# A graph network layer on one core: VectorE's program held behind each turning of edges, and a small first indirect DMA on GpSimd

## The chip, the cores and the metric

The kernel runs on one core of one Trainium2 chip. The metric is the device time of one execution in microseconds. The profiler takes one execution; the engines are called PE (TensorE, matrix products), PEld (its weight loads), DVE (VectorE), ACT (ScalarE), POOL (GpSimd) and SP (SyncE, here a queue of DMAs).

## The reference

A layer for 8192 nodes of 256 channels with 131072 edges, sorted by their destination. Each edge's message is the relu of its source node's row plus a product of its 64 attributes; messages are summed by destination. Beside this local part, attention runs in groups of 32 nodes with 4 heads. A dense stage and a layer norm follow.

```python
ea = edge_attr @ w_e + b_e
msg = jax.nn.relu(x[src] + ea)
agg = jax.ops.segment_sum(msg, dst, num_segments=N)
t = x + agg
h_local = jax.nn.relu(t @ w1 + b1) @ w2 + b2
h_local = _bn(h_local + x, bn1_g, bn1_b)
...
attn = jax.nn.softmax(scores, axis=-1)
...
h_attn = _bn(h_attn + x, bn2_g, bn2_b)
out = h_local + h_attn
out = out + (jax.nn.relu(out @ m_w1 + m_b1) @ m_w2 + m_b2)
return _bn(out, bn3_g, bn3_b)
...
x = _layernorm(x + _L0_gnn_ref(...))
```

## The kernel before

The edges are worked in 128 blocks of 1024 (NB, BE), the nodes in 16 chunks of 512 (NCH, CH). For one block:

- GpSimd gathers the source rows with eight indirect DMAs of 128 rows each into the tile `xs` (line 217). For the first two blocks the row numbers come from the tile `srcd`, loaded at the very start, later from `srci`. For the first 20 blocks the rows come from `x`, later from `xb`, a copy with the edge bias added. Six blocks lack one of the eight gathers; its rows come by SP's queue. There are six buffers of `xs`.
- VectorE turns the block's edge attributes, `eaT` (line 288, `edge_transpose`; two buffers, so a turning waits until PE has used the one before the last).
- PE multiplies them with the weights into two banks `pe` (`edge_products`).
- VectorE adds the gathered rows to `pe` in two halves (line 348, line 342 for the six blocks), ScalarE takes the relu (line 352, `edge_messages`).
- VectorE makes the one-hot tile `oh` from the edges' places in the block (line 363, `edge_hot`, two buffers), PE sums messages by it into `pw`.
- ScalarE copies the sums to `ws`, VectorE makes a second one-hot tile (line 402), PE places the sums, `l`, and VectorE adds them to the chunk's `xT` (line 422, `edge_place`).

For one chunk there is the attention: products of queries, keys and values (`vn`, line 609), scores copied by ScalarE into `pr`, then VectorE's softmax: maximum `mx` (line 635), subtraction (638), exponential on ScalarE (639), sum `sm` (642), reciprocal (643), product (645), four transposes into the tile `bd` (649). PE multiplies `bd` with `vn`. The dense stage has two layers that add to `hA` (lines 672 and 701), two more with `m` and `zT` (lines 707, 719), transposes, the addition to `xn` which gives `y` (732), statistics (734, 735) and the normalisation (742, 744). The last chunk's dense stage is cut by columns (line 775 and on).

What sets the order: PE's order is that of the program text, in which a planner interleaves blocks and chunks by hand-set times. For VectorE and ScalarE the same holds up to block 24 (NV, the flag `stated`). From there on a scheduler of the framework orders them, by its own estimates of when inputs come. `tc.issue_after(ins)` gives it an edge: instructions named inside the context are issued behind `ins` on the same engine. It is an order alone; no engine waits for a semaphore by it. Each gather is also held behind a PE instruction some ten microseconds ahead of it in the planner's time (`hold_fetches`).

Of the kernel before, what the change touches and what calls it, by code (L numbers as in the profile page):

```python
# [19 lines left out]
P = 128  # L20
N, C, E, ED, H, NPG = 8192, 256, 131072, 64, 4, 32
# [3 lines left out]
NB = E // BE  # L25
NH = 4
WN = P // NH
TJ = BE // NH // P
TB = NH * TJ
QR = 32  # L30
EQ = P // QR
# [12 lines left out]
FETCHED = [44, 54, 64, 76, 86, 98]  # L44
# [40 lines left out]
def gnn_kernel(ctx: ExitStack, tc: tile.TileContext, x, src, dst, edge_attr, w, out):  # L85
    nc = tc.nc

    const = ctx.enter_context(tc.tile_pool(name="const", bufs=1))
# [4 lines left out]
    for b in range(ND):  # L93
        for m in range(EQ):
# [24 lines left out]
    rel = const.tile([P, NB, TB], FP, name="rel")  # L119
# [14 lines left out]
    for v in VECS:  # L134
        n = w[v].shape[0] // P
# [92 lines left out]
    xf_of = {}  # L228
# [48 lines left out]
    stated = [True]  # L277
# [2 lines left out]
        for do in spots:  # L280
            do()

    turned_at = [None]

    def edge_transpose(b):
        ea, g0 = ea_of[b // 2], b % 2 * NH * EQ
        eaT = eaT_of[b] = epool.tile([P, NH * EQ, QR], FP, name="eaT", tag="eaT", bufs=2)
        turned_at[0] = nc.vector.transpose(eaT, ea[:, QR:].rearrange("p (g d) -> p g d", d=ED)[:, g0 : g0 + NH * EQ, :QR]).ins  # L288


    pe_of, msg_of, oh_of, pw_of, newest = {}, {}, {}, {}, {}
# [30 lines left out]
    def edge_messages(b, pairs=range(0, NH, 2), of_pair=range(2)):  # L322

        xs = xs_of[b]
        if b not in msg_of:
            msg_of[b] = xs
        msg = msg_of[b]
        n = 2 if b < NB - 1 else 1
        with ExitStack() as behind:
            if not stated[0]:  # L330
                behind.enter_context(tc.issue_after(turned_at[0]))
            for h in pairs:
                pe = pe_of[b, h]
                for u in of_pair[::n]:
                    hs = slice(h + u, h + u + n)
                    if h + u + n == NH and b in FETCHED:
                        for us, js, rows in (
                            (slice(0, 2), slice(0, TJ - 1), xs[:, h:]), (slice(0, 1), slice(TJ - 1, TJ), xs[:, h:]),
                            (slice(1, 2), slice(TJ - 1, TJ), xf_of[b]),
                        ):  # L340
                            rows = rows[:, None, None, :] if rows is xf_of[b] else rows[:, us, js].rearrange("p u i c -> p i u c")
                            nc.vector.tensor_add(
                                msg[:, h:][:, us, js].rearrange("p u i c -> p i u c"), pe[:, js, us, :], rows
                            )
                        nc.scalar.activation(msg[:, hs], msg[:, hs], AF.Relu)
                        continue
                    for js in [slice(0, TJ)] if n == 2 or h + u < NH - 1 else [slice(j, j + 1) for j in range(TJ)]:
                        nc.vector.tensor_add(  # L348
                            msg[:, hs, js].rearrange("p u i c -> p i u c"), pe[:, js, u : u + n, :],
                            xs[:, hs, js].rearrange("p u i c -> p i u c"),  # L350
                        )
                        nc.scalar.activation(msg[:, hs, js], msg[:, hs, js], AF.Relu)  # L352
        between()

    def edge_hot(b):

        oh = oh_of[b] = epool.tile([P, TB, WN], FP, name="oh", tag="oh", bufs=2)
        with ExitStack() as behind:
            if not stated[0]:
                behind.enter_context(tc.issue_after(turned_at[0]))  # L360
            for t0 in range(0, TB, TB // 2):
                ts = slice(t0, t0 + TB // 2)
                nc.vector.tensor_tensor(
                    oh[:, ts],
                    iota_n[:, None, :WN].to_broadcast([P, TB // 2, WN]),
                    rel[:, b, ts, None].to_broadcast([P, TB // 2, WN]),
                    ALU.is_equal,
                )

    def group_sums(pw, i, b, turns):  # L370
        for h, j in turns:
# [58 lines left out]
    with tc.tile_pool(name="setup", bufs=1) as sp:  # L430
# [16 lines left out]
        for v in VECS:  # L447
            r, n = col[v]
# [475 lines left out]
    with tc.manual_schedule(engines={PE}):  # L924
# [39 lines left out]
        for i, c, a, z in (  # L964
# [20 lines left out]
        b = 0  # L985
        while b < TAIL:
# [77 lines left out]
        p, m = [b, 0], [b, 0]  # L1064
# [10 lines left out]
        while l < NB:  # L1075
# [56 lines left out]
            elif t >= times[2]:  # L1132
                i, k = p
# [17 lines left out]
    with tc.If(wide > 0):  # L1151
        with tc.tile_pool(name="gen", bufs=1) as pool, tc.tile_pool(name="gen_ps", bufs=1, space=PSUM) as ps_pool:
# [11 lines left out]
            with tc.For_i(0, E, P * TE) as e0:  # L1164
                ea = pool.tile([P, TE, ED], FP, name="gea")
# [7 lines left out]
                xs = pool.tile([P, TE, C], FP, name="gxs")  # L1173
                for j in range(TE):
                    nc.gpsimd.indirect_dma_start(
                        out=xs[:, j, :],
                        out_offset=None,
                        in_=xb[:, :],
                        in_offset=bass.IndirectOffsetOnAxis(ap=si[:, j : j + 1], axis=0),
                    )  # L1180
                for j in range(TE):
# [9 lines left out]
                    d = df[:, j : j + 1]  # L1191
# [79 lines left out]
```

## Time and profile before

| what | us |
|---|---|
| median of 3 runs (lowest, highest) | 1311.12 (1310.87, 1316.0) |
| the profiled execution, its own time | 1310.63 |
| its span, first to last instruction | 1308.9 |
| mean granted clock of TensorE | 0.966 |
| PE busy | 1200.1 |
| DVE busy | 792.5 |
| POOL busy | 971.1 |
| ACT busy | 581.6 |

A row of a timeline reads: start, duration of the run of equal instructions, engine, line, operation, output and inputs by the program's names, their number, and in brackets the idle time of the engine ahead of it with what ended it. A row of the windows gives for PE, PEld, DVE, ACT and POOL the busy time and the number of instructions, then the granted clock, the DMA engines' share and GB/s. The duration of several instructions is that of the run of them; neighbours on one engine overlap by some 0.1 us. PE's ends are modelled.

### The profile page before, as it was taken

Reading aid. Unit: us, or ns where it says so; the run is one execution under the profiler, and the core shown is the slowest. Engines: PE = TensorE matmul, PEld = TensorE weight load, DVE = VectorE, ACT = ScalarE, POOL = GpSimd, SP = SyncE. Lnnn points to the kernel's source line nnn. Section 1 sums busy time; section 2 is a strip of 40 time slices with the busy share of each in tenths; the row PEclk is TensorE's granted clock in tenths of the full one; section 3 lists DMA queues with packets and bytes.
Section 4 is the critical chain, followed back from the end, with each engine's and each line's share of the span. In section 5 each row is a group of like instructions: output and inputs, shape, how many; then the busy total and the mean of one; then the engine's idle time right before and its main releaser. Section 6 shows DMA issues by size and latency. Waiting matters only on the chain.

```text
span 1308.9 us, 23368 instructions
## 1 busy us (share of the span) xinstructions
PE 1200.1 (92%) x7671; PEld 722.8 (55%) x7671; DVE 792.5 (61%) x1643; ACT 581.6 (44%) x840; POOL 971.1 (74%) x1026
## 2 busy tenths in 40 slices
PE   4997999899979989798998979979889999999997
PEld 3564556555546545555555545545455655556576
DVE  6676856647446565474746638346565765666563
ACT  3443534445526354352544426425245544545343
POOL 6777777777777777777777777777777777777772
PEclk9998999999999989899999989989989999999999
DMA  8999987767768657667687765866777775777642
GB/s 235 290 298 331 285 218 171 166 174 172 187 151 202 155 152 183 163 159 184 155 187 182 175 167 145 190 162 175 183 186 170 189 182 138 202 160 183 150 133 62
DMA packets 146298, 240.53 MB, mean 184 GB/s; under 512 B 24606, under 2 KB 109756, under 8 KB 145404
## 3 DMA queue, kind: packets, MB, share of 16 engines
q0 software_dynamic: 48864, 133.50, 38.1%
q1 hardware_dynamic: 88828, 98.15, 32.4%
q10 hardware_dynamic: 8480, 7.35, 1.9%
q8 instruction: 62, 1.02, 0.3%
q14 instruction: 64, 0.52, 0.1%
HBM read 222.13 MB, written 16.78 MB: 183 GB/s over the span
## 4 chain that ended last, share of the span: by engine, by line
PE 76%; DMA 9%; issue 5%; DVE 4%; POOL 3%; ACT 1%; SPq 0%; DVEq 0%; POOLq 0%; ACTq 0%
PE at L174 38%; PE pe L174 20%; PE pw L174 9%; PE l L174 5%; DMA xs<-xb,srci 4%; POOL xs L217 3%; DVE xs L348 2%; DMA xn<-in_x_dram 2%; DMA xs<-in_x_dram,srci 1%; PE at L775 1%; PE at L178 1%; DMA ea<-in_edge_attr_dram 1%; PE at L726 1%; ACT xs L352 1%; DMA last_src<-in_src_dram 0%
## 5 line engine op out<-in xcount | busy, mean ns | idle before, releaser
L217 POOL DMA_INDIRECT xs<-xb,srci x858 | 815.4, 950 | 262.3 <-issue 181.4
L352 ACT ACTIVATE xs<-xs 128x1024 f32<-128x1024 f32 (+2 forms) x253 | 263.0, 1045 | 434.0 <-DVE xs L348 357.8
L348 DVE TENSOR_TENSOR xs<-pe,xs 128x1024 f32<-128x1024 f32 (+2 forms) x253 | 300.0, 1204 | 211.1 <-PE pe L174 105.4
L174 PE MATMUL pe<-we,eaT 64*128 64x256 f32 x2048 | 271.1, 401 | 10.1 <-DVE xs L348 8.7
L174 PEld LDWEIGHTS pe<-we,eaT 64*128 64x128 f32 x2048 | 196.1, 194 | 108.5 <-issue 66.3
L174 PE MATMUL pw<-xs,oh 128*32 128x256 f32 x2048 | 142.9, 395 | 32.4 <-issue 20.2
L217 POOL DMA_INDIRECT xs<-in_x_dram,srci x144 | 138.6, 962 | 45.2 <-issue 29.3
L174 PEld LDWEIGHTS pw<-xs,oh 128*32 128x32 f32 x2048 | 61.0, 111 | 113.7 <-issue 54.1
L174 PE MATMUL at<-xT,inT 128*128 128x512 f32 x256 | 121.2, 600 | 1.9 <-ACT xT L578 1.9
L174 PE MATMUL at<-hA,mw 128*128 128x512 f32 (+1 forms) x256 | 114.4, 573 | 0.0
L288 DVE STREAM_TRANSPOSE eaT<-ea 128x512 f32<-128x512 f32 x128 | 89.6, 701 | 36.2 <-PE pe L174 31.4
L174 PE MATMUL at<-m,mw 128*128 128x512 f32 (+1 forms) x256 | 108.9, 570 | 0.0
L174 PEld LDWEIGHTS l<-oh,ws 128*128 128x128 f32 x512 | 74.7, 197 | 20.3 <-issue 16.4
L422 DVE TENSOR_TENSOR xT<-l,xT 128x352 f32<-128x352 f32 (+14 forms) x107 | 43.2, 427 | 70.4 <-PE l L174 70.3
L174 PE MATMUL l<-oh,ws 128*128 128x160 f32 (+4 forms) x512 | 85.8, 308 | 0.0
L174 PEld LDWEIGHTS at<-xT,inT 128*128 128x128 f32 x256 | 47.0, 190 | 60.5 <-issue 50.5
L174 PEld LDWEIGHTS at<-m,mw 128*128 128x128 f32 x256 | 47.0, 190 | 46.5 <-issue 42.2
L707 ACT ACTIVATE m<-at,vec 128x512 f32<-128x512 f32 (+1 forms) x64 | 41.8, 655 | 66.3 <-PE at L174 66.2
L174 PEld LDWEIGHTS at<-hA,mw 128*128 128x128 f32 x256 | 46.1, 190 | 44.0 <-issue 41.0
L591 ACT ACTIVATE qk<-at,vec 128x512 f32<-128x512 f32 x64 | 43.8, 685 | 52.9 <-PE at L174 52.5
L174 PE MATMUL pe<-qk 64*128 64x128 f32 x512 | 42.3, 321 | 23.2 <-DVE xs L348 23.2
L174 PE MATMUL at<-oT,outT 128*128 128x512 f32 x128 | 61.5, 604 | 0.3 <-ACT oT L664 0.3
(157 smaller groups left out, 1282.6 us busy)
## 6 DMA issues: line engine op xcount, KB each, us to landing
ea<-in_edge_attr_dram SPq DMA_DIRECT2D x252, 256.0 KB
xs<-xb,srci POOLq DMA_INDIRECT x858
xf<-xb SPq DMA_DIRECT2D x768, 1.0 KB
xn<-in_x_dram ACTq DMA_DIRECT2D x14, 512.0 KB
out_dram<-y SPq DMA_DIRECT2D x14, 512.0 KB
xp<-in_x_dram SPq DMA_DIRECT2D x10, 512.0 KB
xb<-xp SPq DMA_DIRECT2D x10, 512.0 KB
xp<-in_x_dram SPq DMA_DIRECT2D x3, 1024.0 KB
```

The lines of the kernel that those rows point to most:

```text
L174: mark(ps, nc.tensor.matmul(ps, *args, **kw).ins)
L178: ins = nc.tensor.transpose(ps, *args).ins
L217: nc.gpsimd.indirect_dma_start(out=xs[:, h, j, :], out_offset=None, in_=x if b < NX else xb[:, :], in_offset=bass.IndirectOffsetOnAxis(ap= ...
L288: turned_at[0] = nc.vector.transpose(eaT, ea[:, QR:].rearrange("p (g d) -> p g d", d=ED)[:, g0 : g0 + NH * EQ, :QR]).ins
L348: nc.vector.tensor_add(msg[:, hs, js].rearrange("p u i c -> p i u c"), pe[:, js, u : u + n, :], xs[:, hs, js].rearrange("p u i c -> p i u c"),
L352: nc.scalar.activation(msg[:, hs, js], msg[:, hs, js], AF.Relu)
L422: newest["xT"] = nc.vector.tensor_add(xT, l2[:, :, a - n : z - n], xT).ins
L591: nc.scalar.activation(qk[:, o, :], ps, AF.Identity, bias=v_("in_b", o))
L707: newest["relu"] = nc.scalar.activation(m1[:, o, :], layer(mw1, KC, o, hA), AF.Relu, bias=v_("m_b1", o)).ins
L726: nc.tensor.transpose(ps[:wt, t - t2, k * P : (k + 1) * P], zT[:, k, t * P : t * P + wt], ident)
L775: nc.tensor.matmul(ps[i], wt[:, k, o * P : (o + 1) * P], act[:, k, :], start=(k == 0), stop=(k == nk - 1))
```

## The change

There are two edits.

On GpSimd a column of zeros is written, and an indirect DMA by it reads 32 bytes of row 0 for each partition into a tile `first` that nothing reads. Both stand ahead of the identity matrix and the index rows.

On VectorE the edges of issue are laid otherwise. Before, the messages and the first one-hot tile alone were placed behind the newest turning. Now, from block 24 on, a context is opened behind each turning and closed at the next one (after that one has been named itself): every instruction that the program names between two turnings is issued behind the former, and the latter too. No context is opened for the last block.

```diff
+    zero = const.tile([P, 1], I32, name="zero")
+    nc.gpsimd.memset(zero, 0)
+    first = const.tile([P, 8], FP, name="first")
+    nc.gpsimd.indirect_dma_start(
+        out=first, out_offset=None, in_=x.rearrange("n (a b) -> (n a) b", b=8), in_offset=bass.IndirectOffsetOnAxis(ap=zero, axis=0)
+    )
+
     ident = const.tile([P, P], FP, name="ident")
...
-    turned_at = [None]
+    behind_turn = ctx.enter_context(ExitStack())

     def edge_transpose(b):
...
-        turned_at[0] = nc.vector.transpose(eaT, ea[:, QR:].rearrange("p (g d) -> p g d", d=ED)[:, g0 : g0 + NH * EQ, :QR]).ins
+        ins = nc.vector.transpose(eaT, ea[:, QR:].rearrange("p (g d) -> p g d", d=ED)[:, g0 : g0 + NH * EQ, :QR]).ins
+        behind_turn.close()
+        if not stated[0] and b < NB - 1:
+            behind_turn.enter_context(tc.issue_after(ins))
...
     def edge_messages(b, pairs=range(0, NH, 2), of_pair=range(2)):
...
-        with ExitStack() as behind:
-            if not stated[0]:
-                behind.enter_context(tc.issue_after(turned_at[0]))
-            for h in pairs:
+        for h in pairs:
...
     def edge_hot(b):
...
-        with ExitStack() as behind:
-            if not stated[0]:
-                behind.enter_context(tc.issue_after(turned_at[0]))
-            for t0 in range(0, TB, TB // 2):
+        for t0 in range(0, TB, TB // 2):
```

PE's and SP's instructions and their order are the same before and after. GpSimd has two more. VectorE and ScalarE have the same instructions in another order from about 300 us on. Line numbers of the change are four to seven higher than before (the turning 288 is 295, the message add 348 is 355, the first one-hot tile 363 is 367, xT 422 is 426, vn 609 is 613, mx 635 is 639, bd 649 is 653, zT 719 is 723, y 732 is 736).

The first place on VectorE is the softmax at 1104 to 1112 us of the profile before. Before, from the second zT on:

```order
L719 TENSOR_TENSOR zT<-at,zT 128x512
L643 RECIPROCAL sm<-sm 128x16
L645 TENSOR_TENSOR pr<-pr,sm 128x128 x4
L649 STREAM_TRANSPOSE bd<-pr 32x16x32 x4
L288 STREAM_TRANSPOSE eaT<-ea 128x512
L363 TENSOR_TENSOR oh<-iota_n,rel 128x128 x2
L422 TENSOR_TENSOR xT<-l_10516,xT 128x2x144
L348 TENSOR_TENSOR xs<-pe,xs 128x2x2x256 x2
L732 TENSOR_TENSOR y<-at,xn 128x512 x2
```

And in the change, from the second zT on:

```order
L295 STREAM_TRANSPOSE eaT<-ea 128x512
L367 TENSOR_TENSOR oh<-iota_n,rel 128x128 x2
L426 TENSOR_TENSOR xT<-l_10520,xT 128x2x144
L355 TENSOR_TENSOR xs<-pe,xs 128x2x2x256 x2
L639 TENSOR_REDUCE mx<-pr 128x16
L736 TENSOR_TENSOR y<-at,xn 128x512
L642 TENSOR_TENSOR pr<-pr,mx 128x128 x4
L736 TENSOR_TENSOR y<-at,xn 128x512
L738 BN_STATS st<-y 128x6
L646 TENSOR_REDUCE sm<-pr 128x16
```

The turning and the message add now stand ahead of the whole softmax, of which the two y additions and, further on, the statistics have moved in between; `bd` comes nine rows behind the last one shown. The second place is the next softmax, at 1167 to 1178 us, in the change (before, mx and its subtraction stood ahead of the turning, and the second zT behind bd):

```order
L295 STREAM_TRANSPOSE eaT<-ea 128x512
L367 TENSOR_TENSOR oh<-iota_n,rel 128x128 x2
L426 TENSOR_TENSOR xT<-l_10991,xT 128x2x128
L355 TENSOR_TENSOR xs<-pe,xs 128x2x2x256 x2
L639 TENSOR_REDUCE mx<-pr 128x16
L723 TENSOR_TENSOR zT<-at,zT 128x512
L642 TENSOR_TENSOR pr<-pr,mx 128x128 x4
L406 TENSOR_SCALAR oh_11046<-iota_n,wrow 128x128
L723 TENSOR_TENSOR zT<-at,zT 128x512
L646 TENSOR_REDUCE sm<-pr 128x16
```

The third is where the dense stages of the last two chunks meet, at 1245 to 1247 us. In the change, the addition to xT has moved behind the centring `xc`, both reciprocals and the normalisation of two tiles:

```order
L746 RECIPROCAL rstd<-rstd 128x2
L768 TENSOR_TENSOR xc<-xn,c3row 128x256
L748 TENSOR_SCALAR y<-y,mv,rstd 128x256 x2
L746 RECIPROCAL rstd<-rstd 128x4
L426 TENSOR_TENSOR xT<-l_11614,xT 128x2x112
L748 TENSOR_SCALAR y<-y,mv,rstd 128x256 x4
L355 TENSOR_TENSOR xs<-pe,xs 128x2x2x256
```

Before, `xT` stood ahead of the normalisation and of the second reciprocal, and `xc` some fifteen rows earlier.

More of the change, by code (lines that the diff above doesn't have):

```diff
@@ new lines, in edge_messages @@
+        for h in pairs:
+            pe = pe_of[b, h]
+            for u in of_pair[::n]:
+                hs = slice(h + u, h + u + n)
+                if h + u + n == NH and b in FETCHED:
+                    for us, js, rows in (
+                        (slice(0, 2), slice(0, TJ - 1), xs[:, h:]), (slice(0, 1), slice(TJ - 1, TJ), xs[:, h:]),
+                        (slice(1, 2), slice(TJ - 1, TJ), xf_of[b]),
+                    ):
+                        rows = rows[:, None, None, :] if rows is xf_of[b] else rows[:, us, js].rearrange("p u i c -> p i u c")
@@ L353, in edge_messages @@
+                    continue
+                for js in [slice(0, TJ)] if n == 2 or h + u < NH - 1 else [slice(j, j + 1) for j in range(TJ)]:
+                    nc.vector.tensor_add(
+                        msg[:, hs, js].rearrange("p u i c -> p i u c"), pe[:, js, u : u + n, :],
+                        xs[:, hs, js].rearrange("p u i c -> p i u c"),
+                    )
+                    nc.scalar.activation(msg[:, hs, js], msg[:, hs, js], AF.Relu)
         between()
@@ L357, in edge_hot @@
         oh = oh_of[b] = epool.tile([P, TB, WN], FP, name="oh", tag="oh", bufs=2)
-        with ExitStack() as behind:
-            if not stated[0]:
-                behind.enter_context(tc.issue_after(turned_at[0]))
-            for t0 in range(0, TB, TB // 2):
[L362 to L368, printed above, removed]
+        for t0 in range(0, TB, TB // 2):
+            ts = slice(t0, t0 + TB // 2)
+            nc.vector.tensor_tensor(
+                oh[:, ts],
+                iota_n[:, None, :WN].to_broadcast([P, TB // 2, WN]),
+                rel[:, b, ts, None].to_broadcast([P, TB // 2, WN]),
+                ALU.is_equal,
+            )
     def group_sums(pw, i, b, turns):
```

20 lines of the change are left out of this document (2 added, 18 removed).

## The prediction, made before the changed kernel had run

> **What bounds the kernel now.** I read the page first, then the waits of TensorE (PE), a table of windows, the chain of waits, and last the timelines of the places that the new order touches. The page:
>
> ```profile
> PE 1200.1 (92%) x7671; PEld 722.8 (55%) x7671; DVE 792.5 (61%) x1643; ACT 581.6 (44%) x840; POOL 971.1 (74%) x1026
> L217 POOL DMA_INDIRECT xs<-xb,srci x858 | 815.4, 950 | 262.3 <-issue 181.4
> ```
>
> Two engines share the bound. PE is busy 1200.1 of 1308.9 us. GpSimd (POOL) issues the gathers as a metronome: 0.950 us each and 262.3 / 858 = 0.306 us between, 1.256 us a gather, and eight gathers make one block of edges. Where PE idles, this is what it waits for, in the view of waits (us in total, times, longest):
>
> ```profile
> PE pe L174 <- DVE xs L348: 38.4, 20, 5.6
> PE pw L174 <- issue: 20.2, 8, 4.4
> PE pw L174 <- ACT xs L352: 10.2, 3, 4.9
> ```
>
> These 69 us hang on VectorE (DVE): the message adds (xs), ScalarE's relu behind them, and the one-hot tiles (oh) ahead of the group sums (pw). That is the work the change moves. Whether it pays depends on where it lies; the table of windows, PE's busy time first:
>
> ```profile
> 580.00:964.00 384.00, 343.44 (x2112) 202.62 (x2110) 214.45 (x421) 162.40 (x223) 290.83 (x306) 0.95 0.71 172
> 964.00:1082.00 118.00, 117.27 (x768) 67.85 (x766) 80.25 (x165) 63.33 (x91) 89.26 (x94) 0.98 0.75 185
> 1082.00:1309.00 227.00, 215.13 (x1406) 139.06 (x1404) 135.69 (x298) 99.28 (x169) 154.87 (x164) 0.98 0.58 147
> ```
>
> From 580 to 964 PE idles 40.6 us, from 964 to 1082 only 0.7, behind that 11.9. The chain of waits shows where the metronome lets go for the last time:
>
> ```profile
> 1076.17 2.42 DMA xs<-xb,srci
> 1078.61 1.22 DVE xs L348
> 1082.49 1.06 PE pw L174 x12
> ```
>
> A gather lands at 1078.59, its add follows at once, and PE takes up its sums at 1082.49. So PE can't be earlier there than the gathers allow, however well it did before: time won from 300 to 964 is lost again in waiting for this landing. Behind 1082 the chain is PE's own, with DVE in it at a few places, and what is lost there counts in full.
>
> **The change, the GpSimd part.** It adds a small memset and one indirect DMA, and sets the identity and the two index rows behind it. The timeline before, three set-up steps and the first gathers:
>
> ```profile
> 1.00 0.26 POOL L104 IOTA iota_n<- 128x160 f32 x1
> 1.23 0.28 POOL masks.py:199 TENSOR_SCALAR_AFFINE_SELECT ident<-ident 128x128 f32<-128x128 f32 x1
> 1.48 0.13 POOL L106 IOTA iota_p<- 128x1 f32 x1
> 4.30 1.10 POOL L217 DMA_INDIRECT xs<-in_x_dram,srcd  x1 [2.70 <-issue]
> 5.71 0.95 POOL L217 DMA_INDIRECT xs<-in_x_dram,srcd  x1 [0.30 <-issue]
> ```
>
> The first gather takes 0.15 us more than the second, and POOL was idle for 2.70 us ahead of it. The chain of the first microseconds tells what of that is the index load:
>
> ```profile
> 0.76 2.20 DMA srcd<-in_src_dram
> ```
>
> The indices are there at 2.96 at the earliest; 4.30 - 2.96 - 0.30 (the usual pause) = 1.04 us may be a cold start, and with the 0.15 the gain is at most 1.2 us, at least nothing. For a loss: the added DMA and the three set-up steps could, if the whole cold start came ahead of them and nothing of it beside the index load, end at 0.9 + (5.40 - 0.75) + 0.67 = 6.2 us and the first gather start 1.9 us later than 4.30. I take a gain of 0.4, since the idle stretch has room for the added DMA (about 1.3 us) and the setup behind it. A gain here shifts the whole metronome and so the landing at 1078.59.
>
> [...]
>
> **The change, the VectorE part: 300 to 1082.** Each turning of edges (eaT, the transpose of edge attributes) now holds back everything that the program names after it. No instruction is added, and these edges are an order and not a wait. From the blocks at 300 us on DVE's stream changes: the turning, the one-hot tile and the message add move ahead, and copies of values (vn), additions to zT, xT and hA move behind them. One such place:
>
> ```profile
> 940.53 2.35 DVE L348 TENSOR_TENSOR xs<-pe,xs 128x1024 f32<-128x1024 f32 x2
> ```
> ```profile
> 943.77 2.08 PE L174 MATMUL pw<-xs,oh 128*32 128x256 f32 x16 [4.95 <-ACT xs L352]
> ```
>
> PE idles 4.95 us here for a message add that stood behind vn, xT, zT. PE was free at 938.82. In the new order the turning, the one-hot tile and then this add stand ahead of xT and zT, and the turning ahead of vn too; I reckon the add some 5 to 7 us earlier, about as far as the new order pushes the other rows back, so that this wait goes, and so do the like ones of this stretch, most of the 40.6 us. What is pushed back gives PE nothing that it reads in the next steps. I cost the stretch at nothing, for the reason above: its end is set by the landing at 1078.59. If the cover went (the displaced adds holding PE's accumulators, of which there are four), PE would arrive late at 964, where 0.7 us of idle are left until 1082.
>
> **The change, the VectorE part: behind 1082.** Three places are reordered where PE has nothing else to do. First the rule for the attention weights (bd): four transposes, and PE's product with them starts only behind the last:
>
> ```profile
> 1047.39 2.84 DVE L649 STREAM_TRANSPOSE bd<-pr 32x512 f32<-32x512 f32 x4
> ```
> ```profile
> 1050.29 1.97 PE L174 MATMUL at<-bd,vn 128*64 128x128 f32 x32 [0.73 <-DVE bd L649]
> ```
>
> 1047.39 + 2.84 = 1050.23, and PE starts 0.06 later. Place 1, DVE and then PE:
>
> ```profile
> 1111.93 0.71 DVE L288 STREAM_TRANSPOSE eaT<-ea 128x512 f32<-128x512 f32 x1
> 1112.56 0.45 DVE L363 TENSOR_TENSOR oh<-iota_n,rel 128x128 f32<-128x128 f32 x2
> 1112.93 0.45 DVE L422 TENSOR_TENSOR xT<-l,xT 128x288 f32<-128x288 f32 x1
> 1113.30 2.34 DVE L348 TENSOR_TENSOR xs<-pe,xs 128x1024 f32<-128x1024 f32 x2
> 1115.56 1.28 DVE L732 TENSOR_TENSOR y<-at,xn 128x512 f32<-128x512 f32 x2
> 1116.76 0.74 DVE L734 BATCH_NORM_STATS2 st<-y 128x6 f32<-128x256 f32 x2
> ```
> ```profile
> 1106.65 2.00 PE L174 MATMUL pe<-we,eaT 64*128 64x256 f32 x16
> ```
> ```profile
> 1114.66 3.51 PE L174 MATMUL pe<-we,eaT 64*128 64x256 f32 x16 [2.73 <-DVE xs L348]
> 1118.09 1.07 PE L174 MATMUL pw<-xs,oh 128*32 128x256 f32 x16
> 1119.09 1.97 PE L174 MATMUL at<-bd,vn 128*64 128x128 f32 x32
> ```
>
> Before, the softmax ends ahead of the turning, PE pays 2.73 us for the message add, and bd is long there. Now the turning goes first. It needs PE's edge products before it, the 16 of the first PE row, which end at 1108.65, so: turning 1108.7, one-hot and xT until 1110.1, message add until 1112.4. PE's wait of 2.73 goes and its sums end near 1115.1. But softmax now stands behind the add and between the two y adds and the statistics: maximum 0.6, y 0.6, four subtractions 0.85, y 0.6, statistics 0.35 (the exponential of 0.63 on ACT lies beside), sum 0.6, then reciprocal, four products 0.9 and two or three pairs of statistics 0.4 each, 2.15 in all, then 2.85 for bd: 1112.4 + 3.0 + 0.6 + 2.15 + 2.85 = 1121.0. PE starts its product at 1121.05 and not at 1119.09: **+2.0**.
>
> Place 2, the next window's softmax:
>
> ```profile
> 1167.55 0.69 DVE L635 TENSOR_REDUCE mx<-pr 128x16 f32<-128x512 f32 x1 [5.15 <-ACT pr L629]
> 1168.27 0.92 DVE L638 TENSOR_TENSOR pr<-pr,mx 128x128 f32<-128x128 f32 x4
> ```
> ```profile
> 1166.30 2.40 PE L174 MATMUL pe<-we,eaT 64*128 64x256 f32 x16
> ```
> ```profile
> 1169.18 7.03 PE L174 MATMUL at<-m,mw 128*128 128x512 f32 x16
> ```
> ```profile
> 1179.71 1.97 PE L174 MATMUL at<-bd,vn 128*64 128x128 f32 x32
> ```
>
> The maximum now comes behind turning, one-hot, xT and message add (they start when the edge products of 1166.30 end, at 1168.7, and take 3.7 us as at place 1, until 1172.4), and the sum of the exponentials behind the second zT, which needs PE's 16 products of 1169.18, ended at 1176.2. From there zT 0.6, sum 0.6, reciprocal 0.2, products 0.9, bd 2.85: 1181.4, so PE starts at 1181.45 and not at 1179.71: **+1.75**.
>
> Place 3, the first columns of the last dense stage:
>
> ```profile
> 1245.99 0.36 DVE L422 TENSOR_TENSOR xT<-l,xT 128x224 f32<-128x224 f32 x1
> 1246.27 0.73 DVE L744 TENSOR_SCALAR y<-y,mv,rstd 128x256 f32<-128x256 f32 x2
> 1246.91 0.17 DVE L742 RECIPROCAL rstd<-rstd 128x4 f32<-128x4 f32 x1
> ```
> ```profile
> 1246.40 0.71 PE L775 MATMUL at<-xT,w 128*128 128x128 f32 x4 [1.28 <-DVE xT L422]
> ```
>
> PE already waits 1.28 us for the xT add, which now comes behind the y products and the second reciprocal, so it starts at about 1246.94: **+0.95**. The centring of 0.33 (xc) only changes its place ahead of it.
>
> **Sum:** 2.0 + 1.75 + 0.95 = 4.7, less 0.4 at the start, +4.3 us on the profiled execution: its time is 1310.63, 1.73 around a span of 1308.9, so **1314.9 us**. The median of the three runs shown is 1311.12, 0.5 above the profiled one, so against it the forecast is +0.3%. Each of the three could be half or one and a half times as large: 2.4 to 7.1 us.
>
> **Rivals.** (1) As above, 1314.9: 0.55.
> (2) The early message adds win more behind 1082 than softmax loses. For it speaks that the 2.73 at 1114.66 and the 1.28 at 1246.40 are waits for DVE; against it the place of bd. With both gone and no new wait: 1310.63 - 0.4 - 4.0 = 1306.2; but the gathers still land when they did, and I expect a quarter of it, 1309.2: 0.13.
> (3) PE falls behind before 1082, and pays behind it too. Place: 964 to 1082, where PE idles 0.7 us. Mechanism: hA and xT stand behind a turning and a message add which wait for a gather, an accumulator stays taken, PE stops. Price: one pair of adds 2.34 and one turning 0.7, 3.0 us once, on top of the 4.3: 1317.9, twice 1321. It decides as soon as one such hold exceeds the 0.7. Against it: in that stretch few rows change places. 0.20.
> (4) The three places lie beside PE's 11.9 us of idle time behind 1082 and cost nothing: 1310.2. Against it: PE's order stays as it is, and at places 1 and 2 nothing stands between its sums and the product with bd but 1 to 3 us of work. 0.12.
>
> **How the numbers follow.** Half a per cent of the median, 6.6 us, is about what separates a change of this kernel from none. Slower by more than that (over 1317.7) are most of case 3 and the upper end of case 1: 0.17 + 0.05 = 0.22. Faster by more (under 1304.6) is only the far end of 2 and 4: 0.04. The rest, 0.74, is within. Cases 2 and 4 lie at 1309 to 1310, case 3 at 1318 and more; the range that leaves 2 in 10 out is 1309 to 1319.5, and case 1 alone spans 1312.6 to 1317.3.
>
> **What would show it.** The first gather starts near 3.9 and not at 4.30. PE's waits for xs and oh between 580 and 964 shrink by most of their sum, and PE waits for gathers or their adds instead, up to a landing within a microsecond of 1078.6. PE waits for bd, which it did for 0.7 us in all, grow to 5 to 8 us, at two products with bd behind 1110, and for xT to 3 us. The prediction is wrong if PE's idle time from 964 to 1082 rises above 2 us (rival 3), or if the products with bd start where they did (rivals 2 and 4).

## The result and the profile after

| | median us | lowest, highest | ratio to before, 95% interval |
|---|---|---|---|
| before (7 runs) | 1312.44 | 1309.82, 1316.00 | |
| the change (7 runs) | 1322.46 | 1318.11, 1323.46 | 1.0071 [1.0054, 1.0088] |
| the change, measured again beside the last experiments (6 runs; before 1312.17) | 1324.15 | 1319.87, 1327.61 | 1.0089 [1.0067, 1.0110] |

The change is slower by 0.71%, 9.3 us, and by 0.89% in the second measurement. Forecast were 4.3 us and at most 1319.5. The profiled execution of the change took 1322.71 us, with a span of 1320.9.

The table of windows of the changed kernel, with the columns of before (PE's busy time follows the window's length):

```profile
580.00:964.00 384.00, 352.96 (x2209) 205.99 (x2207) 222.04 (x447) 174.26 (x242) 290.82 (x306) 0.97 0.73 176
964.00:1082.00 118.00, 105.72 (x675) 60.97 (x675) 70.67 (x143) 52.67 (x75) 89.19 (x95) 0.97 0.70 177
1082.00:1321.00 239.00, 221.60 (x1422) 142.24 (x1420) 138.79 (x302) 102.12 (x172) 157.78 (x166) 0.98 0.55 141
```

PE does 97 matmuls more than before by 964 us (2209 against 2112), and 93 fewer in the next window: it ran ahead and then idled 12.3 us where it had idled 0.7. The chain of waits of the changed kernel has a gather at the end of this window again:

```profile
1082.14 2.50 DMA xs<-xb,srci
...
1086.27 0.95 ACT xs L359
...
1087.27 1.06 PE pw L181 x12
```

By the chain it landed at 1084.64 and not at 1078.59, and PE takes up the same sums 4.8 us later than before. But that landing held nobody. VectorE's rows show that the message add ahead of these sums had begun at 1083.39, right behind an addition to xT that waited for PE, and the relu followed the add:

```profile
1075.53 1.23 DVE L355 TENSOR_TENSOR xs<-pe,xs 128x1024 f32<-128x1024 f32 x1 [5.61 <-DMA xs<-xb,srci]
...
1083.01 0.46 DVE L426 TENSOR_TENSOR xT<-l,xT 128x288 f32<-128x288 f32 x1 [2.84 <-PE l L181]
1083.39 2.35 DVE L355 TENSOR_TENSOR xs<-pe,xs 128x1024 f32<-128x1024 f32 x2
```

The gather that did hold PE is the one of the first row, some 8 us before that add. The add of this row waited 5.61 us, PE waited 2.89 us for the add, and behind this wait TensorE's granted clock was halved (0.51, the third number from the end of the window's row):

```profile
1076.81 2.04 PE L181 MATMUL pe<-we,eaT 64*128 64x256 f32 x8 [2.89 <-DVE xs L355]
1078.78 1.80 PE L181 MATMUL pw<-xs,oh 128*32 128x256 f32 x16
```
```profile
1076.80:1080.30 3.50, 3.49 (x24) 1.75 (x24) 2.33 (x7) 1.04 (x1) 2.59 (x4) 0.51 0.39 112
```

Eight edge products take 2.04 us here, where sixteen take 2.00 elsewhere, and the sums 1.80 and not 1.07: 1.7 us by the clock. So the time was won between 300 and 964 us and lost again in waiting for gathers, as forecast, and some more was lost with it. The prediction's own row needs the same care. In before, too, the add at 1078.61 stood right behind an addition to xT that waited for PE, so it isn't shown that the landing at 1078.59 held it:

```profile
1078.24 0.46 DVE L422 TENSOR_TENSOR xT<-l,xT 128x288 f32<-128x288 f32 x1 [2.31 <-PE l L174]
1078.61 2.35 DVE L348 TENSOR_TENSOR xs<-pe,xs 128x1024 f32<-128x1024 f32 x2
```

PE's waits, in total, times, longest:

```profile
PE pe L181 <- DVE xs L355: 43.5, 29, 5.7
PE pw L181 <- ACT xs L359: 11.4, 6, 3.3
...
PE at L181 <- DVE bd L653: 9.5, 3, 5.9
...
PE pw L181 <- issue: 2.9, 2, 1.7
```

The wait for one-hot tiles (the sums "pw" that waited for nothing visible) fell from 20.2 to 2.9 us; the wait for bd rose from 0.7 to 9.5.

Place 1, DVE's rows of the softmax and PE's of the product with bd:

```profile
1117.10 0.67 DVE L639 TENSOR_REDUCE mx<-pr 128x16 f32<-128x512 f32 x1
...
1122.74 2.83 DVE L653 STREAM_TRANSPOSE bd<-pr 32x512 f32<-32x512 f32 x4
```
```profile
1116.63 2.00 PE L181 MATMUL pe<-we,eaT 64*128 64x256 f32 x16
1118.56 1.21 PE L181 MATMUL pw<-xs,oh 128*32 128x256 f32 x16
1125.62 3.68 PE L181 MATMUL at<-bd,vn 128*64 128x128 f32 x32 [5.86 <-DVE bd L653]
1129.24 1.33 PE L181 MATMUL l<-oh,ws 128*128 128x144 f32 x4
```

The wait for the message add is gone and PE stands still for 5.86 us ahead of the product with bd. And the product then takes 3.68 us, where the same 32 steps took 1.97 before; the placing products behind it take 1.33 and not 0.76. The windows around it:

```profile
1119.70:1124.60 4.90, 0.07 (x2) 0.00 (x0) 4.87 (x17) 1.85 (x3) 3.87 (x4) 1.00 1.07 261
1124.70:1131.50 6.80, 5.88 (x38) 5.03 (x39) 4.62 (x14) 1.67 (x3) 3.50 (x4) 0.50 0.61 196
1131.50:1137.00 5.50, 5.50 (x44) 3.35 (x44) 3.16 (x6) 4.78 (x7) 3.10 (x4) 1.00 0.28 85
```

TensorE's clock is halved from the end of the idle stretch on, for 6.8 us. That is a cost which the prediction doesn't have.

The start of the changed kernel, first GpSimd's timeline:

```profile
1.61 1.10 POOL L104 DMA_INDIRECT first<-in_x_dram,zero  x1 [0.62 <-POOL ident masks.py:197]
...
4.19 0.96 POOL L224 DMA_INDIRECT xs<-in_x_dram,srcd  x1 [0.76 <-issue]
```
```profile
21.18 0.94 POOL L224 DMA_INDIRECT xs<-in_x_dram,srcd  x1 [1.92 <-PE pe L181]
...
32.11 0.94 POOL L224 DMA_INDIRECT xs<-in_x_dram,srci  x1 [2.50 <-PE at L185]
```

The first gather takes 0.96 and not 1.10 us, and starts 0.11 us earlier: the cold start of 0.15 us has moved to the added DMA (1.10 us). But then the gathers are held behind PE, twice by about 2 us, because PE is late. What PE waits for comes from the loads of the start, here the cast of the source numbers on DVE:

```profile
8.62 1.07 DVE L459 CAST srcf<-srci_r 128x1024 f32<-128x1024 int32 x1 [5.08 <-DMA srci_r<-in_src_dram]
```

It stood at 6.93 before. The windows from 3 to 7 us, of the changed kernel and of before (the last number is GB/s, the one ahead of it the DMA engines' share):

```profile
3.00:5.00 2.00, 0.00 (x0) 0.00 (x0) 0.48 (x3) 0.00 (x0) 1.24 (x4) 1.00 0.48 9
5.00:6.00 1.00, 0.00 (x0) 0.00 (x0) 0.00 (x0) 0.00 (x0) 0.70 (x2) 1.00 1.05 51
```
```profile
3.00:5.00 2.00, 0.00 (x0) 0.00 (x0) 0.48 (x3) 0.00 (x0) 0.70 (x1) 1.00 0.75 57
5.00:6.00 1.00, 0.00 (x0) 0.00 (x0) 0.00 (x0) 0.00 (x0) 0.70 (x2) 1.00 0.91 365
```

In this profile the DMA engines are as busy as before from 5 to 6 us (a share of 1.05 against 0.91), and move 51 GB/s and not 365. The added DMA moves 4 KB: 128 reads of 32 bytes, one for each partition, that all read the same address. The profile has 32 packets of it, of which 24 lie from 4 to 6 us and take 45.3% of the 16 DMA engines' time there; the queue of the loads takes 27.1%, where it took 91.6% before.

### The profile page after: what moved, and what is told of

It reads as the page before. It is cut to its first block, busy times and chain, and to the rows that moved or that the text cites. A ratio compares the mean times of both kernels' runs of the same rounds, so it can differ in the third digit from the quotient of the medians.

```text
span 1320.9 us, 23355 instructions
## 1 busy us (share of the span) xinstructions
PE 1204.1 (91%) x7671; PEld 724.3 (55%) x7671; DVE 792.4 (60%) x1643; ACT 581.2 (44%) x840; POOL 972.7 (74%) x1028
## 4 chain that ended last, share of the span: by engine, by line
PE 64%; DMA 16%; DVE 7%; issue 6%; POOL 4%; ACT 2%; SPq 0%; DVEq 0%; POOLq 0%; ACTq 0%
PE at L181 32%; PE pe L181 16%; DMA xs<-xb,srci 12%; PE pw L181 7%; PE l L181 4%; POOL xs L224 4%; DVE xs L355 3%; DMA xs<-in_x_dram,srci 2%; PE at L779 1%; PE at L185 1%; DVE bd L653 1%; ACT xs L359 1%; PE at L730 1%; DMA last_src<-in_src_dram 1%; DMA ea<-in_edge_attr_dram 1%
## 5 line engine op out<-in xcount | busy, mean ns | idle before, releaser
L181 PE MATMUL pe<-we,eaT 64*128 64x256 f32 x2048 | 267.6, 396 | 14.0 <-DVE xs L355 11.7
L181 PEld LDWEIGHTS pe<-we,eaT 64*128 64x128 f32 x2048 | 192.3, 191 | 112.2 <-issue 56.6
```

The source lines that it names most:

```text
L181: mark(ps, nc.tensor.matmul(ps, *args, **kw).ins)
```

## The experiments

Two theories stood at the start. A: two separate losses, the added DMA at the start and the barrier behind 1082 us. B: the barrier moved the landing at 1082, and the late start was chance. Each run's kernel is given by its difference from the kernel before (or, where said, from the change). Line numbers differ by a few from kernel to kernel; the tiles' names tell which row is which.

**The first four runs** fell on a chip on which the kernel before took 1585.43 us, with a granted clock of 0.92 and many short waits of PE and GpSimd that the others don't have; the ratios of these four, 0.994 to 0.999, tell nothing of 1311 us. The loads of their start agree with the later runs.

The added DMA alone:

```diff
+    zero = const.tile([P, 1], I32, name="zero")
+    nc.gpsimd.memset(zero, 0)
+    first = const.tile([P, 8], FP, name="first")
+    nc.gpsimd.indirect_dma_start(out=first, ...)
     ident = const.tile([P, P], FP, name="ident")
```

> The kernel before with the small first indirect DMA alone; VectorE's order is that of before. Theory A (two separate losses: the added DMA holds up the loads of the start, the barrier costs behind 1082 us alone): 4 to 5 us slower than before; the cast of srci_r near 8.6 us and not 6.9, PE's first edge products near 17 us and not 14.2, and the gathers held for 4 us in all within the first 50. Rival B (the added DMA costs nothing, the start of the changed kernel was late by chance, and the landing at 1082 moved by the barrier between 300 and 1082 us): within 1 us of before, first gather near 4.2 us.

Measured: 0.9988 [0.9970, 1.0006] of 1585.43 us; the cast at 8.73 us, PE's first edge products at 17.04 and a gather held for 2.15 us at 21.53.

The barrier alone (the change without these five lines):

> The change without the small first indirect DMA. Theory A: 6 to 7.5 us slower than before: the three places behind 1082 us (1.7, 1.9 and 1.1 us as the changed kernel's trace has them) and about 2.5 us between the first two; the start as before, the landing at 1078.6 within 1 us. Rival B: 9 to 12 us slower, as the whole change, with the landing 4 to 6 us late.

Measured: 0.9994 [0.9971, 1.0016] of 1585.43; the cast at 7.00, the products at 14.73.

The added DMA with a row of its own for each partition:

```diff
-    zero = const.tile([P, 1], I32, name="zero")
-    nc.gpsimd.memset(zero, 0)
+    each = const.tile([P, 1], I32, name="each")
+    nc.gpsimd.iota(each, pattern=[[0, 1]], base=0, channel_multiplier=32, allow_small_or_imprecise_dtypes=True)
```

> The kernel before with an indirect DMA of 32 bytes a partition at the same place, but each partition reads from a row of its own, so that no two descriptors read the same address. If many reads of one address are what holds up the start: within 1 us of before, the cast of srci_r near 7 us. If any indirect DMA of 128 small descriptors at this time does it: 4 to 5 us slower, as with one address for all.

Measured: 0.9979 [0.9957, 1.0000] of 1585.43; the cast at 6.99, the products at 14.79. So on one and the same chip the start is late with one address for all, and not late with 128 addresses.

The barrier for the early blocks alone, beside the old edges:

```diff
+        behind_turn.close()
+        if not stated[0] and 0 <= b < 104:
+            behind_turn.enter_context(tc.issue_after(turned_at[0]))
```

> The barrier for the turnings of blocks below 104 alone, no added DMA; behind that VectorE's order is that of before. Theory A: within 1 us of before; PE's waits between 580 and 964 us shrink, and it waits for gathers instead up to a landing near 1078.6. Rival B: 4 to 6 us slower, with the landing late by as much.

Measured: 0.9938 [0.9916, 0.9960] of 1585.43 us. There, where PE waits at many other places too, the early turnings are worth 0.6%.

**The next four** ran on a chip like that of the result, with before at 1313.16.

> The kernel before with the added first indirect DMA alone, once more, hoping for a chip on which the kernel before takes about 1311 us; where it takes 1585 the first run of this kernel had its start late as in the changed kernel (srci_r cast at 8.73 us, PE's first edge products at 17.04, gathers held for some 6 us), but the end of such a run is set by other waits. Theory A: 4 to 5 us slower than before. Rival B: within 1 us.

Measured: 1.0014 [1.0001, 1.0027], 1.8 us slower (0.1 to 3.5): less than theory A's 4 to 5, and B's 1 us lies within the interval. The cast at 8.37, a gather held for 2.38 us at 31.35.

> The change without the added DMA, once more. Theory A: 6 to 7.5 us slower than before, the landing near 1078.6 us as before, PE's waits for bd 5 to 9 us. Rival B: 9 to 12 us slower, with the landing 4 to 6 us late.

Measured: 1.0043 [1.0029, 1.0058], 5.7 us slower (3.8 to 7.6): below A's range of 6 to 7.5 in the middle, far from B's 9. The landing is another matter: in this profile PE takes up the sums of 1082 us 5.6 us late (the table below), where A expected them as before and B 4 to 6 us late.

The barrier for the late blocks alone (the lines of above with 104 <= b < NB - 1):

> The barrier for the turnings of blocks 104 and on alone, no added DMA; VectorE's order ahead of 1080 us is that of before. Theory A: as slow as the barrier alone, 6 to 7.5 us over before, with PE's waits for bd and xT. If the barrier costs by what it does between 300 and 1080 us: within 2 us of before.

Measured: 1.0040 [1.0023, 1.0056], 5.2 us slower (3.0 to 7.4).

> The barrier for the turnings of blocks below 104 alone, no added DMA, once more. Theory A: within 1.5 us of before, PE's idle time between 580 and 964 us smaller and in its place waits for gathers up to the same landing near 1078.6. Rival B: 4 to 6 us slower.

Measured: 0.9991 [0.9979, 1.0003], no difference. Its windows and those of the change read alike up to 1082:

```profile
580.00:964.00 384.00, 352.85 (x2206) 205.75 (x2199) 221.68 (x443) 172.25 (x239) 290.35 (x307) 0.97 0.73 177
964.00:1082.00 118.00, 105.87 (x677) 60.72 (x676) 69.89 (x141) 52.04 (x73) 89.37 (x95) 0.97 0.69 172
```

PE ran ahead here too and idled 12.1 us behind 964. So by the times the barrier's loss lies behind block 104, to within some 2 us, and what it wins ahead of it is worth nothing on this chip. Theory B, by which this kernel would be 4 to 6 us slower, has fallen.

**Place 1.** In the table that follows each number is the start of one PE instruction less the start of the same instruction in the profile of before, at the time of before that heads the column; the PE order is the same in all (twelve added products left out). The difference from column to column is what a stretch costs in that one execution. The profile of before took 1310.63 us, 1.8 less than its median, so against a usual execution of before each row stands some 2 us too high.

```
                         964   1082.4    1093     1100    1113    1119    1121.5   1179.5   1181.5   1244   1246.3    1250    end
the change             -10.10   4.77     4.77     4.77    1.97    6.53     8.77     8.93    10.91   11.17   12.08   12.08   12.08
the change, again      -10.26   2.86     2.86     2.86    0.06    4.66     6.90     6.91     8.89    9.19   10.09   10.09   10.08
barrier alone          -10.76   5.57     5.57     5.57    2.77    7.39     9.17     8.77    10.75   11.07   11.97   11.97   11.96
barrier from 104         1.26   0.93     1.16     5.75    2.95    7.51     9.75     9.41    11.38   11.69   12.59   12.59   12.58
barrier from 104 again   0.33  -0.33    -0.10     4.02    1.22    5.78     8.02     8.04    10.02   10.28   11.19   11.19   11.18
place 1 filled          -0.97  -2.13    -1.91     4.00    1.20    5.79     5.79     5.38     7.36    7.62    8.59    8.59    8.59
place 1 filled, again    0.78   0.72     0.71     0.71   -2.09    2.48     2.48     2.09     4.09    4.48    5.46    6.94    6.93
place 1 undone          -1.83  -1.77    -1.54     0.58    0.59    0.75     0.75     1.38     4.04    4.93    5.91    7.56    7.56
barrier to 104         -11.80   3.20     3.20     3.20    3.21    3.18     3.18     3.18     3.18    3.18    3.19    3.19    3.18
```

From 1100 to 1119, place 1 costs 1.8 us in all seven executions that have it (4.77 to 6.53 in the change), place 2 (1179.5 to 1181.5) 2.0, place 3 (1244 to 1246.3) 0.9. Between 1119 and 1121.5 lie the product with bd and its slow clock: 1.8 to 2.2 us where PE had idled 5.9 us, nothing where the idle stretch is filled.

Between 1093 and 1100 lie 2 to 6 us more in four rows. There PE's sums wait for a message add that waits for a gather, in the first run of the filled kernel:

```profile
1091.72 1.22 DVE L352 TENSOR_TENSOR xs<-pe,xs 128x1024 f32<-128x1024 f32 x1 [5.75 <-DMA xs<-xb,srci]
```

The wait is only a part of it. PE's rows in the same execution:

```profile
1094.09 1.92 PE L174 MATMUL pw<-xs,oh 128*32 128x256 f32 x12 [2.62 <-ACT xs L356]
1095.94 3.79 PE L174 MATMUL pe<-we,eaT 64*128 64x256 f32 x16
```

Twelve sums take 1.06 and sixteen products 2.00 us in before, so 2.7 us of the 5.9 come in slower products behind the wait. These executions had reached 1082 with little or no delay. So had the second run of the filled kernel, which loses nothing here. Whether the barrier has a part in this loss stays open. On these chips every execution that loses 2 us or more here has the barrier behind block 104, but one and the same kernel, the filled one, loses 5.9 us in one execution and nothing in the other.

The idle stretch of place 1 was filled with products that nothing reads, in the bank that the product with bd overwrites:

```diff
             ps = bank()
+            if st is chunk[14] and not k:
+                for _ in range(12):
+                    nc.tensor.matmul(ps[:, :C], ident, vn[:, 0, :], start=True, stop=True)
```

> The barrier from block 104 on, and twelve products that nothing reads (identity by vn, 128 by 256, into the bank that the product with bd then overwrites) put into PE's idle stretch ahead of the late product with bd; all other orders as with the barrier from 104 on. If the idle stretch lowers the clock: the idle time ahead of the product falls from 5.9 to some 2.6 us, its 32 steps take about 2.0 us and not 3.68, the granted clock there is 1.0 and not 0.50, and the kernel is 2 to 2.7 us faster than with the barrier from 104 on, so 2.5 to 3.5 us slower than before. If the product was slow for another reason (bd's landing, weights, contention with GpSimd): still 3.7 us, and no gain.

Measured: 1.0034 [1.0021, 1.0047], 4.5 us slower (2.8 to 6.2) where 2.5 to 3.5 was expected. The PE timeline of this kernel at place 1:

```profile
1118.93 5.45 PE L660 MATMUL at<-vn,ident 128*128 128x256 f32 x24
1124.88 1.97 PE L174 MATMUL at<-bd,vn 128*64 128x128 f32 x32 [0.50 <-DVE bd L653]
```

The product takes 1.97 us again. The twelve products took 5.45 us and not 3.3, and so fill nearly the whole stretch. In time the kernel came out 0.06%, 0.8 us, below the barrier from 104 on, and not the 2 to 2.7 us expected; the two had been measured apart, so both ran once more side by side:

> The barrier from block 104 on, once more, as the base of the filled kernel: 4 to 7 us slower than before, the product with bd 3.7 us long at a granted clock of 0.50.

Measured: 1.0047 [1.0031, 1.0063], 6.2 us slower (4.1 to 8.3); the product took 3.68 us.

> The same with the idle stretch filled. If the slower clock costs what the trace shows (2.2 to 2.5 us): 1.5 to 3 us faster than the barrier from 104 on in this call. If its loss is taken back by waits behind it: within 1 us of it.

Measured: 1.0042 [1.0026, 1.0057], 0.6 us less, with intervals that cover each other. In this execution 1.5 us come back between 1246.3 and 1250; in the first run of the same kernel nothing does (8.59 in all of the last columns). The windows of the filled kernel there:

```profile
1249.00:1252.00 3.00, 0.98 (x6) 0.66 (x5) 3.00 (x15) 0.77 (x2) 2.39 (x3) 0.92 0.42 116
1252.00:1255.00 3.00, 3.00 (x11) 2.64 (x12) 2.63 (x7) 0.54 (x2) 2.23 (x3) 0.51 0.72 212
```

At place 3 PE idles 2.0 of 3 us in two pieces, and here the clock falls to 0.51 behind them. In the change it didn't, with gaps as long (1.00 from 1256 to 1261, gaps of 1.24 and 0.71 us), and the first run of this same kernel has no loss there in the table. PE's rows:

```profile
1250.48 0.67 PE L174 MATMUL l<-oh,ws 128*128 128x112 f32 x4 [1.31 <-DVE rstd L749]
1251.86 1.22 PE L782 MATMUL at<-xT,w 128*128 128x128 f32 x4 [0.71 <-DVE xT L426]
1252.88 1.91 PE L174 MATMUL at<-xT,w 128*128 128x256 f32 x4
```

The last took 1.03 in the change. So the clock's part at place 1 is shown by the trace, and a gain in time from filling it isn't.

Place 1 was undone by leaving the turning of block 111 out of the barrier:

> The barrier from block 104 on, but not behind the turning of block 111: VectorE has the order of before again at the softmax near 1104 to 1122 us, and the changed order at the two later places. Theory A (place 1 costs twice, by bd coming 1.8 us late and by about 2.5 us of a slower TensorE clock behind an idle stretch of 5.9 us): 2 to 3.5 us slower than before where the barrier from 104 on is 5.2 (3.0 to 7.4) slower; no wait of PE above 3 us behind 1085 us and a granted clock of 1.0 around the product with bd. If the clock has nothing to do with it: 3.5 to 5 us slower.

Measured: 1.0041 [1.0025, 1.0057], 5.4 us slower (3.3 to 7.5), no gain either; the expectation failed. The edit did what was meant: VectorE's order differs from that of the barrier from 104 on at place 1 alone, and place 1 costs only 0.2 us here (0.58 to 0.75). But the slow clock came at other places. At place 2 PE idles 1.91 us ahead of the product with bd, which takes 2.64 us at a clock of 0.50:

```profile
1183.08 2.64 PE L174 MATMUL at<-bd,vn 128*64 128x128 f32 x32 [1.91 <-DVE bd L653]
```
```profile
1184.30:1187.60 3.30, 3.30 (x24) 2.64 (x20) 3.13 (x4) 2.45 (x4) 2.35 (x3) 0.50 0.37 112
```

The second run of the barrier from 104 on has the same gap there, and neither the slow product nor the slow clock:

```profile
1189.74 1.97 PE L174 MATMUL at<-bd,vn 128*64 128x128 f32 x32 [1.91 <-DVE bd L653]
```
```profile
1188.00:1194.00 6.00, 4.26 (x52) 3.80 (x54) 5.94 (x11) 2.89 (x4) 4.70 (x5) 1.00 0.39 112
```

So place 2 costs 2.7 us here and the stretch to 1244 0.9, and a slow clock at place 3 (0.50 from 1252.5 to 1255.8) another 1.65. Two ways of taking place 1's cost away, filling and undoing, thus changed the trace as meant and left the time where it was. That place 1's 1.8 and 2.2 us are worth as much in the kernel's time isn't shown.

**The address.** The kernel before with the spread DMA, on the faster chip:

> The kernel before with the added first indirect DMA, each partition reading a row of its own. If many reads of one address hold up the loads of the start, and that is worth the 1.8 us (0.1 to 3.5) that the added DMA alone cost: within 0.7 us of before, or up to 0.7 faster, srci_r cast near 7.0 us, no gather held before 30 us. If the address has no part in it: 1 to 3 us slower.

Measured: 1.0004 [0.9994, 1.0015]. DVE's cast and the window from 5 to 6 us:

```profile
6.81 1.07 DVE L462 CAST srcf<-srci_r 128x1024 f32<-128x1024 int32 x1 [3.27 <-DMA srci_r<-in_src_dram]
```
```profile
5.00:6.00 1.00, 0.00 (x0) 0.00 (x0) 0.00 (x0) 0.00 (x0) 0.69 (x2) 1.00 0.96 379
```

379 GB/s, where one address left 51: the same number of reads of the same size at the same place. In all four profiles with one address 42 to 62 GB/s pass from 5 to 6 us and the cast starts at 8.33 to 8.73; in the fourteen others it is 362 to 389 and 6.72 to 7.38. What held up the start in these profiles is the one address. What that is worth in time is less clear: 1.0014 and 1.0004 have intervals that cover each other.

Both edits without the parts that cost:

> The barrier for turnings below block 104 and the added DMA with a row of its own for each partition: both edits without the parts that cost. Theory A: the gathers start up to 0.5 us earlier and the rest is bound by them as before, so 0 to 1.5 us faster than before; not over 1 us slower.

Measured: 1.0023 [1.0011, 1.0034], 3.0 us slower than before where it was expected level or faster. Of its profile's 4.2 us at the end, 2.75 are there at 1082 and 1.2 more by 1119; but the barrier to 104 without the DMA has 3.2 at 1082, and it isn't slower. Why the spread DMA costs here and not alone stays open.

The whole change, and the whole change with the spread DMA, side by side:

> The whole change, once more, beside the other kernels of this call: 7 to 11 us slower than before.

Measured: 1.0089 [1.0067, 1.0110].

> The whole change with a row of its own for each partition in the added DMA. If the one address is what the added DMA costs, also in the presence of the barrier: as slow as the barrier alone, 4 to 7 us over before, 2 to 4 us faster than the whole change, srci_r cast near 6.9 us. If the rest of the difference is something else in the start: as slow as the whole change.

Measured: 1.0074 [1.0052, 1.0097], 2.0 us below the change, with intervals that overlap; the expectation, as slow as the barrier alone, failed. The cast stood at 7.38, where 6.9 was expected. Against the barrier alone (1.0043, measured apart) there remain 4 us that the address doesn't explain. The barrier to 104 says the same: the spread DMA added to it costs 4.2 us (from 1.2 faster to 3.0 slower), while added to the kernel before it costs 0.5. So one address is worth 1 to 2 us of the 9 to 12 at the middle of both comparisons (1.0014 to 1.0004, 1.0089 to 1.0074), and neither tells it from nothing. Beside the early barrier an added DMA of either kind costs some 4 us or more (3.6 and 6.0 with one address, 4.1 and 4.2 without), each a difference of ratios from different chips with some 2 us either way, and the cause of that isn't settled. No version here beats the kernel before; the barrier to 104 equals it.

## Why the prediction was wrong

**What failed in the sum is the term for the start, and a term for the clock that it doesn't have.** By the times it is the start: in place of a gain of 0.4 us the added DMA cost 1.8 alone and 3.6 beside the barrier (9.3 less 5.7), while the barrier's 4.7 lies within the interval of each measurement of it. By the traces the clock's term was missing as well. Point by point:

- "I take a gain of 0.4, since the idle stretch has room for the added DMA": wrong in sign. The instruction did fit, it ended at 2.71 us, and the cold 0.15 us moved with it (1.10 us for it, 0.96 for the first gather). But the bounds were drawn on GpSimd's own time alone; the packets of the added DMA were still in the DMA engines when the loads of the start went through, 45.3% of these engines' time from 4 to 6 us. The price came by another way than the bounds: srci_r 1.7 us late, PE's first products 2.9, and then the gathers, which are held behind PE, by 4.4 us some fifty gathers on in the change's profile (from 67.8 to 72.2) and by 2.1 in its second one. Alone it measured +1.8 us. That my own range of a loss, up to 1.9, holds this number is luck, its mechanism was another. And the late start is not the whole price: beside the early barrier a DMA that leaves the start nearly alone costs some 4 us too, for a reason that no run here shows.
- Place 1, 2 and 3, "+2.0, +1.75, +0.95": measured 1.8, 2.0 and 0.9 in the trace of the change. The rule from one row of before, that the product with bd starts behind its last transpose (1125.57 to 1125.62 here), carried two of them. They are sizes in the trace; that undoing place 1 brings its share back in time wasn't shown.
- Missing: the clock. The same working that made the product with bd late left PE standing for 5.9 us, and the prediction didn't ask what a stretch without work does to TensorE. The trace of before had the answer on two rows that the prediction quotes: the sums behind the idle 4.95 us at 943.77 took 2.08 us, where such sums take 1.07 elsewhere, and at place 1 itself the edge products behind the idle 2.73 us at 1114.66 took 3.51 and not 2.00. The granted clock of before there:

```profile
943.70:947.00 3.30, 3.23 (x22) 2.17 (x24) 0.17 (x1) 0.27 (x1) 2.39 (x4) 0.50 0.76 201
1114.40:1117.70 3.30, 3.04 (x14) 2.71 (x16) 3.30 (x8) 3.00 (x4) 2.39 (x4) 0.50 1.08 243
```

  By the table the slow clock takes 1.8 to 2.2 us at place 1; a gain in time from removing it wasn't shown (0.6 us, with intervals that cover each other). At place 1 of the change the clock was 0.50 for 6.8 us behind 5.86 us of idle time, then 1.00. It was 0.50 behind shorter stretches too: 2.73 us of idle time in before, 1.91 in the kernel with place 1 undone.
- 300 to 1082, "I cost the stretch at nothing": right in time, 0.9991 [0.9979, 1.0003], and PE was 10 to 12 us early at 964 in all kernels with the early barrier and had lost it all at 1082 to gathers, as the prediction said. It did not see that such a wait can lose more than was won: 1.7 us by the halved clock in the change's profile.
- Sum by the traces: 1.8 + 2.2 + 2.0 + 0.9 = 6.9 for the barrier, measured at 5.2, 5.7 and 6.2 in the three measurements of it (alone, and twice from 104 on), each with some 2 us either way; with the start's 1.8 it is 8.7, of 9.3 measured (7.1 to 11.6) and 11.7 in the second measurement.
- Of the rivals, (3) put the place wrongly: PE's idle time from 964 to 1082 did rise far above 2 us, to 12.3, which by the prediction's own test would have spoken for it. But it was PE come early and waiting for gathers, not PE fallen behind. The test couldn't tell the two apart; the count of matmuls in the window can.
- The landing at 1078.6 "within a microsecond": the chain has 1084.6, which held nobody, and the add at 1078.61 in before hadn't been shown to wait for its landing either. PE came to these sums 4.8 us late. The held gathers may have a part in that, but the barrier alone, whose start isn't late, comes there 5.6 us late in its profile. By the table the same instruction at 1082 lies 2.1 us before to 5.6 behind that of before's profile in kernels that should agree. One profile against another couldn't have been read to better than some 3 us.

## What to carry to other kernels

A wait that is moved onto PE has two prices, the wait and the half clock that can follow (0.50 behind 5.86 us at place 1 of the change; behind 1.91 us at place 2, 0.50 in one kernel and 1.00 in another); look in the trace of before for products that follow a gap and compare their duration with the same products elsewhere. A slow product that goes from one place can come back at another (3.68 us at place 1 with the barrier from 104 on, 2.64 us at place 2 with place 1 undone), so a price read from one trace is not yet a gain in time. An added DMA is costed by what it does in the DMA engines beside the loads that are under way, not by its instruction's row; one that only warms up should read rows of its own, not one address for all partitions, as far as the loads of this start show (379 against 51 GB/s from 5 to 6 us). A chain of waits names what came last, and that can be a landing that nobody waited for: see whether the engine had been idle. An edge that only sets an order can still reorder a whole scheduled stretch: read the order where PE has no slack, and look there for what is now between a product and its last input.

## What the runs showed of the hardware

With 128 reads of 32 bytes from one address the transfer rate of all queues from 5 to 6 us was 51 GB/s and not 365 (42 to 62 in the four profiles that have it), and the cast that waits for the 512 KB of srci_r came 1.4 to 1.8 us later; with the same 128 from rows 1 KB apart it was 379 GB/s. The granted clock fell to 0.50 behind 5.86 us without products in the change and behind 2.73 us in before. Behind 1.91 us it was 0.50 in one kernel and 1.00 in another with the same gap, and behind two gaps close together it was 0.51 in one execution of the filled kernel (1.31 and 0.71 us) and 1.00 in the change (1.24 and 0.71 us). So in these traces the length of a gap alone doesn't tell whether the clock halves.
